# Layer 0 of a four-layer graph network: the last 20 nodes' attention weights turned by TensorE instead of by VectorE blocks and DMAs

## The chip, the cores and the metric

The kernel runs on one core of a Trainium2 chip. The metric is device time in microseconds, the median of several runs; every execution is one launch of the whole program. The engines are named as in the profile: PE is TensorE (PEld its weight loads), DVE VectorE, ACT ScalarE, POOL GpSimd, SP SyncE, which here only issues DMAs.

## The reference

A graph of 2708 nodes with 512 features each passes through four layers. Every layer is followed by a residual and a layer norm: `x = layernorm(x + layer(x, adj))`. Layer 0, the only one that the change touches, is attention with 8 heads of 64, masked by the adjacency matrix:

```python
keys    = einsum('nj,hjk->hnk', x, Wks)
queries = einsum('nj,hjk->hnk', x, Wqs)
values  = einsum('nj,hjk->hnk', x, Wvs)
atts = einsum('hqk,hmk->hqm', queries, keys) / 64**0.5
atts = softmax(atts - 1e16 * (1 - max(adj, eye)), axis=-1)
out  = einsum('hqm,hmk,hko->qo', atts, values, Wo)
```

Layers 1 to 3 are two graph convolutions and an additive graph attention. All data are float32.

## The kernel before, in words

**Tiles.** The nodes are cut into 22 chunks of 128 (`NC`), the last with 20 nodes (`LR`). Keys lie transposed in `KT`, values in `V` (128 nodes of a chunk on the partitions, 512 values in the free dimension). Layer 0 works through 85 items: for each of the first 21 chunks of queries four pairs of heads (class `Pair`), and one item (class `Last`, item 84) for the 20 queries of the last chunk with all eight heads, four groups of 32 partitions side by side. The keys of an item are taken in three batches: chunks 0 to 7, 8 to 15 and 16 to 21 (`ends`, `ND` = 16).

**The steps of an item.** `scores` (PE products into `pss`, DVE adds the mask and takes maxima into `s`), `weights` (ACT's exponential in place on `s`, with the row sums by the accumulator), and then the weights have to be turned, so that the keys lie on the partitions. For batches 0 and 1 this is done in two steps: `blocks` (two DVE transposes of 32x32 blocks from `s` into a tile `d`, L380) and `deal` (four DMAs, one for each group of 32 partitions, from `d` into a tile `e`, L390). That leaves the keys of a chunk in another order, partition 4x+i for key 32i+x, and the values of the first 16 chunks are computed in that order as well: POOL permutes x before the projection (L264). For batch 2 `turn` uses PE transposes into PSUM (`pst`, L409 to L418), copied by ACT to `pt`, `pt2` and `lastT`. `values` then multiplies with `V` (L436) into `av`, or for `Last` into four banks `avz`, and `finish` copies the result out of PSUM (L456, or L500 to `otz`) and stores it in DRAM from POOL's queue (`otd`, L457, L501).

**The order.** For PE, DVE and ACT the order is written out by hand (`manual_schedule`): in step i of the loop the newest item gets its scores, the one before (`cur`) its weights and turns, and the ones before that (`late`, `old`) their values, a batch at a time. In the step after the last item's scores, `cur` is the last item, `late` item 83 and `old` item 82. SP's and POOL's order isn't written out; a planner chooses it. Tiles `d` have two buffers, tiles `e` three; the PSUM tags `s0` and `s1` have two banks each and hold the scores' products and later `avz`.

**Behind the items.** `heads_rows` and `last_sums` turn the reciprocals of the row sums (PE `prs`, `prz`), copy them by ACT (L524, L535, one buffer `rst`) and store them from POOL (L525, L536). Then the output projection: for every chunk SP loads the stored values (`otl`, L683), x (L684) and the reciprocals (`rb`, L692), Wo having been loaded once (L113), POOL multiplies (L693), PE projects (`po`, L696), and DVE adds x (L697) and does the layer norm.

Of the kernel before, what the change touches and what calls it, by code (L numbers as in the profile page):

```python
# [8 lines left out]
F32 = mybir.dt.float32  # L9
AF = mybir.ActivationFunctionType  # L10
# [5 lines left out]
P = 128  # L16
BLK = 512
# [5 lines left out]
def kernel(  # L23
# [22 lines left out]
    nc = tc.nc  # L46
# [11 lines left out]
    def cols(b):  # L58
        return b * BLK, min(BLK, N - b * BLK)
# [11 lines left out]
    ident = const.tile([P, P], F32, tag="ident", name="ident")  # L71
# [45 lines left out]
    ends = [0, 8, 16, NC]  # L117
    ND = ends[2]
    KD4 = P // 32
# [16 lines left out]
    FILL = 32 - LR  # L136
    otd = [dram.tile([P, NP, rows(c)[1]], F32, tag=f"otd{c}", name=f"otd{c}") for c in range(NC)]
    with ExitStack() as l0:
# [12 lines left out]
        def batch(k):  # L151

            n0 = ends[k] * P
            return n0, min(ends[k + 1] * P, N) - n0
# [54 lines left out]
        with tc.tile_pool(name="kvw", bufs=1) as kvw, tc.tile_pool(name="xTb", bufs=2) as xtp, tc.tile_pool(  # L209
            name="ps_0", bufs=4, space=PSUM  # L210
# [4 lines left out]
            for b in range(NB):  # L215
                n0, w = cols(b)
# [86 lines left out]
        ps_s = l0.enter_context(tc.tile_pool(name="ps_s", bufs=2, space=PSUM, reuse_waits="tile"))  # L303
        sp = l0.enter_context(tc.tile_pool(name="sp", bufs=5, reuse_waits="tile"))
        dp = l0.enter_context(tc.tile_pool(name="dp", bufs=2, reuse_waits="tile"))
        ep = l0.enter_context(tc.tile_pool(name="ep", bufs=3, reuse_waits="tile"))
        ptp = l0.enter_context(tc.tile_pool(name="ptp", bufs=1, reuse_waits="tile"))

        class Pair:
# [58 lines left out]
            def weights(self, k):  # L368

                w = batch(k)[1]  # L370
                for j in range(2):
                    s = self.s[k][:, j, :w]
                    nc.scalar.activation(s, s, AF.Exp, bias=self.nm[j], accum_out=self.sums(j, k))  # L373

            def blocks(self, k, j):

                n = ends[k + 1] - ends[k]
                if k not in self.D:
                    self.D[k] = dp.tile([P, KD4, 2, n, 32], F32, tag="d", name=f"d{self.c}_{self.p}_{k}")
                nc.vector.transpose(  # L380
                    self.D[k][:, :, j].rearrange("p i m x -> p m i x"),
                    self.s[k][:, j, : n * P].rearrange("p (m i x) -> p m i x", i=KD4, x=32),
                )

            def deal(self, k):

                n = ends[k + 1] - ends[k]
                e = ep.tile([P, KD4, 2, n, 32], F32, tag="e", name=f"e{self.c}_{self.p}_{k}")
                for g in range(KD4):
                    nc.sync.dma_start(  # L390
                        e[:, g].rearrange("p j m x -> p (j m x)"),
                        self.D[k][32 * g : 32 * g + 32].rearrange("p i j m x -> p i (j m x)"),
                    )
                self.E[ends[k]] = e
# [30 lines left out]
            def weight(self, m, j):  # L425

                if m >= ND:
                    return self.pts[m, j]
                f = max(f for f in self.E if f <= m)
                return self.E[f][:, :, j, m - f, :]  # L430
# [28 lines left out]
        class Last(Pair):  # L459
# [19 lines left out]
            def weight(self, m, p, j):  # L479
                if m >= ND:  # L480
                    return self.pts[m, j][:, 32 * p + FILL : 32 * p + 32]
                f = max(f for f in self.E if f <= m)
                return self.E[f][:, p, j, m - f, FILL:]

            def values(self, m0, m1):
                if self.done == 0:
# [54 lines left out]
        with tc.manual_schedule(  # L541
            engines={mybir.EngineType.PE, mybir.EngineType.DVE, mybir.EngineType.Activation}
        ):
            for i in range(len(items) + 3):
# [4 lines left out]
                if i < len(items):  # L549
                    c, p = items[i]  # L550
# [559 lines left out]
    with tc.tile_pool(name="zp", bufs=2) as zp:  # L1110
# [44 lines left out]
        def banks(name):  # L1155
            return [ps_acc.tile([P, BLK], F32, tag="acc", name=f"{name}_{k}") for k in range(FC)]
# [41 lines left out]
        w = cols(TAIL)[1]  # L1198
# [22 lines left out]
        while n0 < NH * P:  # L1221
            w = min(BLK, NH * P - n0)
            n1 = NH * P + n0
            nchunks = w // P
            j = n0 // BLK
# [26 lines left out]
            m4, m7, e = banks(f"m4_{j}"), banks(f"m7_{j}"), banks(f"e0_{j}")  # L1252
# [13 lines left out]
            m3, m6, e = banks(f"m3_{j}"), banks(f"m6_{j}"), banks(f"e1_{j}")  # L1266
# [61 lines left out]
```

## Time and profile before

| | |
|---|---|
| median of 3 runs | 2588.55 us (2586.21 to 2588.58) |
| the profiled execution | 2589.45 us, its span 2587.7 us |
| PE busy | 2532.2 us, 98% of the span |
| DVE busy | 1874.8 us, 72% |
| ACT busy | 1211.7 us, 47% |
| mean granted clock of PE | 0.991 |
| layer 0's items on PE | to 1253.5 us; the output projection from 1256.6 us |

The page names engine, line, operation, output and inputs of each group; times in a timeline are from the start of the span. The square bracket at the end of a timeline's row is the idle time of the engine before it and what ended it; "issue" is waiting for nothing that the profile shows. In the windows the columns are the length of the window, then busy time and number of instructions of PE, PEld, DVE, ACT and POOL, then the granted clock, the DMA engines' mean busy share and GB/s.

### The profile page before, as it was taken

To read this page: it belongs to the slowest core of one execution; us is meant where nothing else is said; L and a number is where in the kernel's file an instruction comes from. 1 tells how busy PE (TensorE), PEld (TensorE's weight loads), DVE (VectorE), ACT (ScalarE), POOL (GpSimd) and SP (SyncE) were. 2 spreads that over 40 slices of the span, in tenths; PEclk is the share of its full clock that TensorE was granted. 3 is DMA by queue.
4 is the path that set the end of the run, shared out by engine and by line. 5 is a ranking of instruction groups with operands and counts; after the bars stand their busy time and mean duration, and the time that the engine had idled before them with its cause. 6 is when DMAs were issued, how large, how long until landed. Compare 5 with 4: busy or idle time off the path is not lost.

```text
span 2587.7 us, 42022 instructions
## 1 busy us (share of the span) xinstructions
PE 2532.2 (98%) x15263; PEld 1468.0 (57%) x15263; DVE 1874.8 (72%) x4576; ACT 1211.7 (47%) x2417; POOL 314.0 (12%) x322
## 2 busy tenths in 40 slices
PE   9999999999999999999899999899999999999997
PEld 4445676766776767676556444444444466444465
DVE  2004999999999999999484777988776874443544
ACT  2113878788787787887111001565665640000000
POOL 2110000000000000000220000343333430000000
PEclk9999999999999999999899999999999999999999
DMA  5112888888888888888763444454433213644633
GB/s 201 33 54 69 217 233 212 232 216 213 234 212 212 233 213 222 225 210 199 215 201 87 125 124 145 119 158 137 124 108 116 64 31 111 186 139 144 178 102 106
DMA packets 221499, 411.42 MB, mean 159 GB/s; under 512 B 28765, under 2 KB 48911, under 8 KB 221292
## 3 DMA queue, kind: packets, MB, share of 16 engines
q1 hardware_dynamic: 215052, 392.00, 55.5%
q0 software_dynamic: 6240, 16.73, 1.7%
q8 instruction: 121, 1.98, 0.3%
q14 instruction: 86, 0.70, 0.1%
HBM read 213.55 MB, written 16.72 MB: 89 GB/s over the span
## 4 chain that ended last, share of the span: by engine, by line
PE 79%; issue 9%; DVE 7%; DMA 2%; ACT 1%; SPq 1%; POOL 0%; POOLq 0%; DVEq 0%; ACTq 0%
PE pss L329 15%; PE av L436 15%; PE acc L750 13%; PE acc L856 7%; PE m L1160 6%; PE pf L762 3%; PE psv L269 3%; PE pst L409 3%; PE psq L230 3%; PE psk L230 2%; PE ph L842 1%; PE acc_0a L750 1%; DVE d L380 1%; DMA e<-d 1%; DVE s L351 1%
## 5 line engine op out<-in xcount | busy, mean ns | idle before, releaser
L351 DVE CUSTOM_DVE_ANT_0 s<-pss,adj 128x512 f32<-128x512 f32 (+1 forms) x1020 | 574.5, 619 | 27.3 <-PE pss L329 25.4
L373 ACT ACTIVATE s<-s,nm 128x1024 f32<-128x1024 f32 (+1 forms) x510 | 527.7, 1037 | 17.3 <-DVE nm L366 15.5
L329 PE MATMUL pss<-KT,qt 64*128 64x512 f32 (+1 forms) x2016 | 459.5, 565 | 4.0 <-DVE mx L351 3.9
L380 DVE STREAM_TRANSPOSE d<-s 128x1024 f32<-128x1024 f32 x340 | 402.4, 1222 | 9.4 <-DMA e<-d 6.5
L750 PE MATMUL acc<-pt,x 128*128 128x512 f32 (+1 forms) x880 | 336.2, 541 | 9.7 <-ACT pt L803 9.7
L436 PEld LDWEIGHTS av<-e,V 128*64 128x64 f32 x5376 | 294.6, 137 | 62.7 <-DMA e<-d 46.2
L436 PE MATMUL av<-e,V 128*64 128x128 f32 x5376 | 326.3, 274 | 0.0
L329 PEld LDWEIGHTS pss<-KT,qt 64*128 64x128 f32 x2016 | 191.1, 186 | 139.9 <-issue 67.2
L750 PEld LDWEIGHTS acc<-pt,x 128*128 128x128 f32 x880 | 159.4, 194 | 186.1 <-issue 162.8
L856 PE MATMUL acc<-at,h 128*128 128x512 f32 (+1 forms) x504 | 196.8, 543 | 0.0
L814 POOL TENSOR_TENSOR cs<-cs,pt 128x512 f32<-128x512 f32 (+2 forms) x110 | 157.6, 1433 | 202.2 <-ACT pt L803 199.8
L801 DVE TENSOR_TENSOR pt<-pt,at 128x512 f32<-128x512 f32 (+2 forms) x132 | 109.0, 833 | 76.4 <-ACT pt L800 76.2
L457 POOL DMA_DIRECT2D otd<-ot x84 | 45.3, 540 | 954.9 <-ACT ot L456 942.5
L1190 ACT ACTIVATE z<-pz,rdeg 128x512 f32<-128x512 f32 (+1 forms) x22 | 15.1, 688 | 311.5 <-PE pz L762 311.5
L93 ACT ACTIVATE ln_t<-lnve 128x1 f32<-128x1 f32 x88 | 17.7, 201 | 305.3 <-DVE lnve L107 305.2
L856 PEld LDWEIGHTS acc<-at,h 128*128 128x128 f32 x504 | 90.2, 190 | 101.4 <-issue 99.0
L410 ACT COPY pt<-pst 128x512 f32<-128x512 f32 x170 | 91.5, 589 | 120.0 <-PE pst L409 119.8
L436 PEld LDWEIGHTS av<-pt,V 128*64 128x64 f32 x1680 | 90.0, 136 | 64.6 <-ACT adj L187 46.2
L803 ACT ACTIVATE pt<-pt 128x512 f32<-128x512 f32 (+2 forms) x132 | 76.1, 579 | 102.8 <-DVE pt L802 102.6
L867 DVE SCALAR_TENSOR_TENSOR cs<-at,rdeg,cs 128x512 f32<-128x512 f32 (+2 forms) x126 | 86.2, 684 | 41.9 <-DMA at<-in_adjT_dram 40.9
L436 PE MATMUL av<-pt,V 128*64 128x128 f32 x1680 | 110.3, 278 | 1.4 <-ACT ot L456 1.4
L85 DVE COPY KT<-psk 128x512 f32<-128x512 f32 (+1 forms) x12 | 7.5, 629 | 131.6 <-PE psk L230 113.9
(299 smaller groups left out, 3563.7 us busy)
## 6 DMA issues: line engine op xcount, KB each, us to landing
e<-d SPq DMA_DIRECT2D x680, 256.0 KB
at<-in_adjT_dram SPq DMA_DIRECT2D x210, 256.0 KB
a<-in_adj_dram SPq DMA_DIRECT2D x38, 677.0 KB
adj<-in_adj_dram SPq DMA_DIRECT2D x42, 512.0 KB
at_a<-in_adjT_dram SPq DMA_DIRECT2D x40, 256.0 KB
at_c<-in_adjT_dram SPq DMA_DIRECT2D x40, 256.0 KB
at_f<-in_adjT_dram SPq DMA_DIRECT2D x40, 256.0 KB
adj<-in_adj_dram SPq DMA_DIRECT2D x21, 330.0 KB
```

The source lines that it names most:

```text
L230: nc.tensor.matmul(ps[:, :w], w_sb[:, k, p * P : (p + 1) * P], xb[:, k, :w], start=(k == 0), stop=(k == KC - 1),)
L329: nc.tensor.matmul(pss[j][:, :w], qt[h, self.p, :], KT[h, self.p, n0 : n0 + w], start=True, stop=True)
L351: nc.vector.tensor_tensor_reduce(out=s[:, j, h0 : h0 + hw], in0=pss[j][:, :hw], in1=a[:, n0 + h0 : n0 + h0 + hw], scale=1.0, scalar=LOW, o ...
L373: nc.scalar.activation(s, s, AF.Exp, bias=self.nm[j], accum_out=self.sums(j, k))
L380: nc.vector.transpose(self.D[k][:, :, j].rearrange("p i m x -> p m i x"), self.s[k][:, j, : n * P].rearrange("p (m i x) -> p m i x", i=KD4 ...
L410: nc.scalar.copy(sb, pt)
L436: nc.tensor.matmul(self.av[j * KD : (j + 1) * KD, out], V[:, m, h * KD : (h + 1) * KD], weights[j], start=(self.done == 0), stop=(self.don ...
L750: nc.tensor.matmul(acc[k][:, :w], last[0][g : g + mr, :] if m == NC - 1 else values[:mr, k * P : (k + 1) * P], moving[g : g + mr, :w], sta ...
L801: nc.vector.tensor_tensor(pt[:mr, :w], pt[:mr, :w], at[:mr, :w], ALU.subtract)
L814: nc.gpsimd.tensor_tensor(sums[:mr, :w], sums[:mr, :w], pt[:mr, :w], ALU.add)
L856: nc.tensor.matmul(acc[hc][:, :w], lastH[g : g + mr, :] if m == NC - 1 else H[m][:mr, hc * P : (hc + 1) * P], at[g : g + mr, :w], start=(m ...
L1160: nc.tensor.matmul(acc[k][:, : moving.shape[1]], combined[which, m][:, k * P : (k + 1) * P], moving, start=(m == 0), stop=(stop and m == N ...
```

## The change

Only the class `Last` changes, and in it only batches 0 and 1. `weights` lets ACT write the exponentials into a tile `d` of shape queries x 2 x chunks x 128, with key 32i+x of a chunk at place 4x+i, the order in which `V` has the values. `blocks` does nothing. `deal` issues no DMA: it transposes each 128x128 piece of `d` on PE, four to a PSUM bank (tags `s0`, `s1`), and DVE copies each bank into `e`. `weight` takes its 20 columns from the new layout. Batch 2 is as before.

```diff
                 f = max(f for f in self.E if f <= m)
-                return self.E[f][:, p, j, m - f, FILL:]
+                return self.E[f][:, j, m - f, 32 * p + FILL : 32 * p + 32]
+
+            def weights(self, k):
+
+                w = batch(k)[1]
+                n = ends[k + 1] - ends[k]
+                if ends[k] >= ND:
+                    return Pair.weights(self, k)
+                self.D[k] = dp.tile([P, 2, n, P], F32, tag="d", name=f"dz_{k}")
+                for j in range(2):
+                    nc.scalar.activation(
+                        self.D[k][:, j].rearrange("p m (x i) -> p m i x", i=KD4),
+                        self.s[k][:, j, :w].rearrange("p (m i x) -> p m i x", i=KD4, x=32),
+                        AF.Exp,
+                        bias=self.nm[j],
+                        accum_out=self.sums(j, k),
+                    )
+
+            def blocks(self, k, j):
+                pass
+
+            def deal(self, k):
+
+                n = ends[k + 1] - ends[k]
+                e = ep.tile([P, 2, n, P], F32, tag="e", name=f"ez_{k}")
+                for j in range(2):
+                    for m0 in range(0, n, 4):
+                        pt = ps_s.tile([P, BLK], F32, tag=f"s{j}", name=f"psz{k}_{j}_{m0}")
+                        for i in range(4):
+                            nc.tensor.transpose(pt[:, i * P : (i + 1) * P], self.D[k][:, j, m0 + i, :], ident)
+                        nc.vector.tensor_copy(e[:, j, m0 : m0 + 4, :], pt)
+                self.E[ends[k]] = e
```

## The prediction

> **What bounds the kernel now.** I read the page first, for the engine that carries the span.
>
> ```profile
> PE 2532.2 (98%) x15263; PEld 1468.0 (57%) x15263; DVE 1874.8 (72%) x4576; ACT 1211.7 (47%) x2417; POOL 314.0 (12%) x322
> q8 instruction: 121, 1.98, 0.3%
> ```
>
> TensorE is busy nearly everywhere, so what is gained on its path at one place stays gained. The change touches one of 85 work items, the last one of layer 0, so the question is what ends the time between 1227 and 1262 us. For that I read the chain of waits there.
>
> ```profile
> 1223.46 5.91 DMA e<-d
> 1229.50 2.38 DVE d L380 x2
> ...
> 1239.01 0.63 SPq L390
> 1239.68 2.96 SPq L113
> 1242.88 6.66 DMA otl<-otd
> 1249.62 5.57 DMA otl<-otd
> 1255.19 1.36 POOL otl L693
> 1256.59 9.10 PE po L696 x16
> ```
>
> SP's queue is full of the shuffles e<-d until 1239.64; only then does it issue Wo and the blocks for the output projection. Next, TensorE in order of time, and the granted clock microsecond by microsecond.
>
> ```profile
> 1239.74 3.71 PE L436 MATMUL avz<-e,V 128*64 128x20 f32 x121
> 1245.14 0.41 PE L436 MATMUL avz<-e,V 128*64 128x20 f32 x7 [1.69 <-issue]
> ...
> 1245.83 5.72 PE L436 MATMUL avz<-e,V 128*64 128x20 f32 x118
> 1252.65 0.83 PE L436 MATMUL avz<-e,V 128*64 128x20 f32 x10 [1.09 <-issue]
> 1256.59 19.45 PE L696 MATMUL po<-wo_sb,otl 128*128 128x512 f32 x40 [3.12 <-POOL otl L693]
> ```
>
> ```profile
> 1246.00:1247.00 1.00, 1.00 (x38) 1.00 (x38) 0.00 (x0) 0.09 (x1) 0.54 (x1) 0.95 1.01 350
> 1247.00:1248.00 1.00, 1.00 (x25) 1.00 (x22) 0.00 (x0) 0.00 (x0) 0.00 (x0) 0.50 1.17 344
> 1260.00:1261.00 1.00, 1.00 (x3) 0.53 (x2) 0.00 (x0) 0.00 (x0) 0.00 (x0) 0.72 0.00 0
> ```
>
> The last item's values stop twice for nothing a semaphore shows. The stops lie 128 matmuls apart (121 | 7 + 2 + 118 | 10), that is 256 instructions with the weight loads, and the 30526 PE instructions over the 121 packets of the q8 instruction queue (packets, MB, share) are about 252 each: these are instruction fetches, late while the DMA engines are full (share 1.0). After the first stop the clock falls to 0.50 at about 1246.9 and returns at about 1260.6. Then TensorE idles 3.12 us. POOL, in order, says why:
>
> ```profile
> 1253.94 0.52 POOL L536 DMA_DIRECT2D rz_d<-rstz  x1 [7.01 <-ACT otz L500]
> 1254.46 0.78 POOL L501 DMA_DIRECT2D otd<-otz  x1
> 1255.19 3.96 POOL L693 TENSOR_TENSOR otl<-otl,rb 128x512 f32<-128x512 f32 x3
> ```
>
> The first product for the projection stands behind two DMA issues that wait for the last item's end (ACT copies otz at 1253.56).
>
> **Removed.** Four DVE block transposes (L380, 1.22 us each; DVE has idle time there), eight DMAs of 256 KB, and SP's issues of them (1231.93 to 1239.64). So SP reaches Wo (L113) right behind item 83's shuffles, near 1229 instead of 1239.68; nothing in the trace makes Wo wait for more. Wo, three otl, three rb and three x are about 3.3 MB, issued in 13 us in the trace; they should be issued by 1242 and land by about 1245, where before they filled the engines until 1255.5.
>
> **Added, ACT.** The exponentials of batches 0 and 1 now write into the d buffers, so they wait until item 83's shuffles have read those. The trace shows when: DVE's transposes, which need the same buffers, start at 1229.50 and 1233.22 after waiting 1.84 and 1.35 us for DMA e<-d. ACT starts batch 0 at 1229.5 instead of 1227.65 and batch 1 at 1233.2 instead of 1230.07. Behind them on ACT stand the copy ot of item 82 (TensorE's av bank waits for it), the third batch and the copies pt. Four ACTIVATEs write with a step of four elements. No ACT row has that. Lower end: L373 itself, 1.14 us each with the accumulator read. Upper end: POOL's permuting copies of x (L264), 4.13 us for four with a step against 2.29 us for four straight, 1.8 times, so 2.05 us each. I take 1.14, the row of the same engine and operation; the upper end makes the item 1.9 us later (followed through the chain below). [...]
>
> **Added, PE and DVE.** 32 transposes. Row L409 has 8 in 1.02 us in the chain, so 16 per batch cost 2.05 us, all on TensorE's path. Eight DVE copies of 128x512 out of PSUM at 0.69 us (L85), 5.5 us, lie on an idle DVE beside TensorE's next work; their banks (tags s0, s1) are free after the last scores at 1227.4, and the last item's avz waits for the second batch's copies, done near 1239.0, before it starts.
>
> **TensorE step by step.** Item 82's values end at 1228.8 as now. Transposes of batch 0 from 1230.7 (first exponential) to 1232.9 (second at 1231.7, plus eight transposes). Item 83's values, 3.2 us: 1236.1 (now they start at 1230.21). Batch 1's transposes, whose exponentials are ready at 1235.5: 1238.15. Twelve pst transposes, 1.46: 1239.6. Item 83's rest, 1.75: 1241.35. The last item from pt and lastT, 2.77: 1244.1. Then 128 matmuls at 3.71/121, 3.93: 1248.05; prs and prz 0.35; 128 more, 3.93: 1252.35. Now they end at 1253.48: 1.1 us earlier, although the item's values start 4.4 us later, because the two stops and the half clock are taken out.
>
> **Behind it.** With the loads landed by 1245, POOL's first three L693 can be issued ahead of L536 and L501, as readiness orders POOL (it is not among the engines whose order is written by hand). Then the projection follows avz without the 3.12 us, and at full clock: its first 16 matmuls took 9.10 us, where 66 later ones took 28.52 us (0.432 each, 6.9 for 16), 2.2 us lost now. From there the stage is TensorE's, 176 matmuls by 0.432, so its start moves its end. Next late could be otz's copies (po1 and po2 reuse banks of avz), which only need to come within po0's 3.4 us.
>
> Sum: -1.1 - 3.1 - 2.2 = -6.4. For one late fetch in place of two I give back 0.5: -5.9. The profiled execution took 2589.45 us (span 2587.7), so it would take 2583.55; it lies 0.9 above the median of 2588.55, which goes to 2582.65, say 2582.7. A difference of 0.2%, 5.2 us, is about what a measurement of this kernel can tell from no change.
>
> [...] The trace holds no window of transposes alone: in each item 12 of them, 1.46 us, lie between other matmuls, at clock 1.00; one stop of 1.69 us among avz was enough for 0.50. In the new order TensorE idles from 1228.8 to 1230.7 and then only transposes for 2.05 us; later it transposes for 3.5 us on end. [...]
>
> **Rivals.**
> First: POOL keeps its order. L693 stays behind L501; only the 1.1 us and part of the slow start come off, and TensorE still idles about 3.2 us. For: SP and POOL are ordered by what the planner takes as ready, not by the trace. Against: the loads move about ten microseconds ahead of the two DMA issues. Time: 1 to 3 less, 2586.5.
> Second, slower: the clock falls between 1233 and 1240. At 0.50 the trace has 82 avz matmuls from 1246.95 to 1251.4, 54 ns each against 30.7; 352 of them cost 8.3 us more, and the transposes and item 83's values (5.3 us) up to 4 more if the drop comes first. avz then ends at 1260.6 to 1264, and the projection starts there cold instead of at 1256.59: 4 to 8 us slower, about 2594.5. [...]
> Third: ACT's stepped writes at 2.05 us: 1.9 us of the gain go, about 2584.5; with another step of TensorE late, less.
>
> **How the numbers follow.** Forecast case 0.48, first rival 0.24, second 0.20, third 0.08. Faster by over 0.2%: 0.85 of the forecast case (0.41), a little of the first and third (0.03): 0.44. Slower: 0.65 of the second (0.13), and 0.04 for both a late POOL and a cold clock: 0.17. The rest, 0.39, is within. Low end: the forecast with no late fetch and 3 us for later waits that an earlier start may meet better, 2579.5. High end: the second rival's nearer half, 2593. The forecast's own range is 2580 to 2585.
>
> **What would show it.** Right: SP issues Wo near 1229; avz runs without a stop at clock 1.0 and ends near 1252; L693 stands before L501 on POOL; po follows avz within 0.5 us and its first 16 matmuls take about 7 us. Wrong: PEclk 0.50 in the windows from 1233 on (second rival); L693 behind L501 with a PE gap near 3 us (first); ACTIVATEs with output d at 2 us (third). If the exponentials wait past 1233.2 because Wo's load slows item 83's shuffles, every step behind them slips by as much.

## The result and the profile after

The kernel after takes 2590.46 us (median of 22 runs, 2586.32 to 2597.29) where the kernel before, beside it, takes 2586.85 us (22 runs, 2581.12 to 2590.67). The ratio is 1.0016, 95% interval 1.001 to 1.0022: slower by 3.6 us, not faster by 5.9. (The ratio is worked out over the runs and isn't the quotient of the two medians; the same holds for the tables below.) The profiled execution of the kernel after took 2592.34 us, its span is 2590.5 us.

Two lines of the page answer to the first ones of before:

```profile
PE 2535.0 (98%) x15295; PEld 1470.1 (57%) x15295; DVE 1874.1 (72%) x4580; ACT 1214.6 (47%) x2417; POOL 313.7 (12%) x322
q8 instruction: 121, 1.98, 0.3%
```

TensorE has 32 matmuls and 32 weight loads more, the 32 turns. The instruction queue q8, which I take to bring its code, still moves 121 pieces. This will matter. In order of time, ScalarE, the queues and TensorE in the stretch that the prediction worked on (line numbers behind about 515 are 31 higher than before; this execution stands 1.95 us behind that of before already at 1221, where the two programs are still the same, so 1.95 is to be taken off each start):

```profile
1231.55 2.09 ACT L493 ACTIVATE dz<-s,nm 128x1024 f32<-128x1024 f32 x1 [1.86 <-DMA e<-d]
1235.90 2.19 ACT L493 ACTIVATE dz<-s,nm 128x1024 f32<-128x1024 f32 x1
```

```profile
1233.70 3.65 PE L512 MATMUL psz<-ident,dz 128*128 128x128 f32 x16 [2.91 <-ACT dz L493]
1237.28 1.31 PE L436 MATMUL av<-pt,V 128*64 128x128 f32 x20
...
1240.48 1.97 PE L512 MATMUL psz<-ident,dz 128*128 128x128 f32 x16
...
1248.26 3.89 PE L436 MATMUL avz<-ez,V 128*64 128x20 f32 x128
...
1252.43 3.92 PE L436 MATMUL avz<-ez,V 128*64 128x20 f32 x128
1256.66 5.82 PE L727 MATMUL po<-wo_sb,otl 128*128 128x512 f32 x13 [0.32 <-issue]
```

Batch 0's exponentials start when item 83's shuffles give the d buffers back, as foreseen; the row of batch 1's shows no such wait, ScalarE only comes to it then. Each takes 2.1 us and not 1.14. TensorE stands still for 2.91 us ahead of the first turned batch, and turns it in 3.65 us where the second takes 1.97. The windows say why (us, busy times and counts by engine, then the granted clock, the DMA share and GB/s):

```profile
1229.00:1233.00 4.00, 1.78 (x32) 1.54 (x30) 0.61 (x4) 2.14 (x4) 0.00 (x0) 1.00 0.86 239
1233.60:1236.80 3.20, 3.07 (x13) 2.67 (x14) 1.38 (x2) 3.06 (x6) 0.54 (x1) 0.50 0.88 246
1237.00:1256.00 19.00, 19.00 (x468) 18.17 (x467) 4.77 (x10) 7.36 (x18) 2.91 (x4) 1.00 0.55 156
```

After the stop the clock is at 0.50 for 3.41 us, from 1233.46 to 1236.87, then at 1.00 through avz. In the clock records of this profile and of that of before every fall that ends within the span lasts 3.41, 6.83 or 13.65 us, and the starts of the falls of one record lie whole multiples of 3.413 us apart; such a stretch of 3.41 us is called a window of the clock below. SP's issue of Wo and, of POOL, the last item's issues beside the products for the projection:

```profile
1231.47 0.61 SPq L113 DMA_DIRECT2D wo_sb<-in_wo_dram  x1
1253.54 1.28 POOL L724 TENSOR_TENSOR otl<-otl,rb 128x512 f32<-128x512 f32 x1
1255.41 0.55 POOL L567 DMA_DIRECT2D rz_d<-rstz  x1 [0.59 <-ACT otz L531]
1256.87 0.74 POOL L532 DMA_DIRECT2D otd<-otz  x1 [0.91 <-ACT otz L531]
```

So most of what was foreseen came: Wo issued early, avz without a stop, the projection 0.32 us behind it and at full clock. From 1221 to the start of layer 1 (1367) this execution gains 4.2 us on that of before. By 2383, in layer 3, it is only 0.3 us ahead, with falls of the clock in layers 1 and 2 at other places than before (1666.9, 1728.4, 1824.0 and 2100.4 us; there 1653.1, 1670.2, 1731.6, 2008.1 and 2100.2), and there it loses 2.8 us at one spot, where the order of the instructions is the same. TensorE there, in the kernel before and in the kernel after:

```profile
2393.00 1.99 PE L1160 MATMUL m<-jb,x 128*128 128x512 f32 x4 [1.64 <-DVE jb L1152]
```

```profile
2393.82 3.65 PE L1191 MATMUL m<-jb,x 128*128 128x512 f32 x4 [2.79 <-DVE jb L1183]
```

The stop is 1.15 us longer and the four matmuls behind it run at half clock. VectorE's wait for the block at_c is behind it, before and after:

```profile
2392.05 0.29 DVE L1147 TENSOR_TENSOR at_c<-at_c,ident 128x128 f32<-128x128 f32 x1 [1.97 <-DMA at_c<-in_adjT_dram]
```

```profile
2392.87 0.29 DVE L1178 TENSOR_TENSOR at_c<-at_c,ident 128x128 f32<-128x128 f32 x1 [3.11 <-DMA at_c<-in_adjT_dram]
```

And the DMA queues between 2388 and 2393 (packets, MB, share of 16 engines), before and after:

```profile
q1 hardware_dynamic: 660, 1.20, 77.4%
q0 software_dynamic: 80, 0.26, 13.1%
```

```profile
q1 hardware_dynamic: 611, 1.10, 72.7%
q0 software_dynamic: 80, 0.26, 13.4%
q8 instruction: 1, 0.02, 1.8%
```

One piece of q8 travels beside at_c in the kernel after (from 2389.4 on, for 1.45 us), and none in the kernel before. That became the theory, called C in the texts below; A and B are told in the first of them.

To compare executions, the tables below give two differences to the first profile of the kernel before, each between the starts of the same VectorE instruction. The stretch goes from item 83's last score blocks (1221.0 there) to layer 1's first h (1367.2). The spot goes from a sum y of layer 3 (2382.9) to the product jc (2405.4). Less than zero is a gain. A further profile of the kernel before gives -2.0 and -0.4, so 2 us in the stretch between two single profiles are no finding.

### The profile page after: what moved, and what is told of

It is laid out like the page before. It is cut to its first block, busy times and chain, and to the rows that moved or that the text cites. A ratio compares the mean times of both kernels' runs of the same rounds, so it can differ in the third digit from the quotient of the medians.

```text
span 2590.5 us, 42086 instructions
## 1 busy us (share of the span) xinstructions
PE 2535.0 (98%) x15295; PEld 1470.1 (57%) x15295; DVE 1874.1 (72%) x4580; ACT 1214.6 (47%) x2417; POOL 313.7 (12%) x322
## 3 DMA queue, kind: packets, MB, share of 16 engines
q8 instruction: 121, 1.98, 0.3%
## 4 chain that ended last, share of the span: by engine, by line
PE 80%; issue 9%; DVE 6%; DMA 2%; ACT 1%; SPq 1%; POOL 0%; POOLq 0%; DVEq 0%; ACTq 0%
PE pss L329 15%; PE av L436 15%; PE acc L781 13%; PE acc L887 7%; PE m L1191 6%; PE pf L793 3%; PE psv L269 3%; PE pst L409 3%; PE psq L230 3%; PE po L727 3%; PE psk L230 2%; PE ph L873 2%; DVE s L351 1%; DVE d L380 1%; DMA e<-d 1%
## 5 line engine op out<-in xcount | busy, mean ns | idle before, releaser
L380 DVE STREAM_TRANSPOSE d<-s 128x1024 f32<-128x1024 f32 x336 | 397.6, 1221 | 8.0 <-DMA e<-d 3.0
```

The lines of the kernel that those rows point to most:

```text
L380: nc.vector.transpose(self.D[k][:, :, j].rearrange("p i m x -> p m i x"), self.s[k][:, j, : n * P].rearrange("p (m i x) -> p m i x", i=KD4 ...
```

## The experiments

All kernels of a batch ran on one chip together with the kernel before.

### The two kernels again, and the two halves of the wait

The kernel before again and the kernel after again; the exponentials in the score buffers, so that they don't wait for item 83's shuffles; and the exponentials written straight, without the values' order, so that the last 20 nodes' weights meet the wrong values:

```
-self.D[k] = dp.tile([P, 2, n, P], F32, tag="d", name=f"dz_{k}")
+self.D[k] = sp.tile([P, 2, n, P], F32, tag="s", name=f"dz_{k}")      # third run

-self.D[k][:, j].rearrange("p m (x i) -> p m i x", i=KD4),
-self.s[k][:, j, :w].rearrange("p (m i x) -> p m i x", i=KD4, x=32),
+self.D[k][:, j].rearrange("p m x -> p (m x)"),                      # fourth run
+self.s[k][:, j, :w],
```

> The kernel before once more, for its spread and for a second profile of it. Theory A (the clock's windows): the stretch of the last item is faster by 4 to 5 us in the changed kernel, but what follows then lies otherwise against fixed windows of 3.41 us, and more of the 2-us stops of layers 1 to 3 end in half clock. If the windows are fixed to the start of the execution, this profile shows the half clock at the same places as the first one (1247, 1653, 1670, 1731, 2008, 2100 us, give or take 1); if they run free, at others. Theory B (the stretch itself): the stretch of the last item is slower in most executions than in the one profiled, and the rest does not matter. Both: ratio 1.000, within 0.001.

> The changed kernel once more. Both: 1.001 to 1.002 of before. A: from item 83's values to the first layer norm of layer 1 it gains 4 to 5 us on the kernel before again, and it has lost 4 us or more against that by the end, at places where the granted clock is 0.50 in this kernel and 1.00 in the kernel before. B: the stretch gains less than 1 us or loses, and from there to the end the two kernels run alike within 1 us.

> The exponentials go into tiles of the tag s, which are free by then, and not into the d buffers, which item 83's shuffles still read. ACT starts batch 0 behind the copies of item 83 (1.9 us earlier), TensorE's stop before the first transposes falls from 2.9 to about 1 us and its clock stays at 1.00 there; the stretch ends 2 to 3 us earlier than in the changed kernel. B: the total falls by the same 2 to 3 us, to 1.0004. A: the total changes by that and by what the windows then do, anything from -6 to +3 us against the changed kernel.

> The exponentials are written in the order in which they are read; the 20 last nodes' weights then meet the wrong values, so this one's output is not the reference's. It takes the step of four elements away. ACT's four ACTIVATEs take 1.14 us instead of 2.1; batch 0's second one ends 1 us earlier, and the stretch ends 1 to 2 us earlier than in the changed kernel. B: the total falls by 1 to 2 us. A: by that and by what the windows do, -5 to +4 us.

| kernel | median us (runs) | ratio, interval | stretch | spot |
|---|---|---|---|---|
| before again | 2586.11 (11) | 0.9993, 0.9985 to 1.0002 | -2.0 | -0.4 |
| after again | 2589.59 (11) | 1.0009, 1.0 to 1.0018 | +0.3 | +3.2 |
| score buffers | 2590.80 (12) | 1.0004, 0.9992 to 1.0016 | -5.8 | +2.6 |
| straight | 2587.31 (11) | 0.9997, 0.9988 to 1.0006 | -5.2 | +2.8 |

The kernel before had a median of 2587.42 beside them. Its second profile has half clock from 1243.6, 1666.9 and 1728.3 on and none at 1653, 2008 or 2100, where the first has it: the falls differ between executions of one kernel. The second profile of the kernel after gains nothing in the stretch: half clock lies there at 1233.9 for two windows, at 1257.8 and at 1339.7. Written straight, the exponentials take 1.15 us, so the step makes the 2.1. With either half of the wait gone the stretch gains what was foreseen, 5 to 6 us, in the profile. Yet the medians don't show it, and the profiles of the kernel after and of both versions lose 2.6 to 3.2 us at the same spot of layer 3. The twelve times with the score buffers fall into two groups, five of 2582.7 to 2586.6, the profiled one among them, and seven of 2589.8 to 2595.4. Every execution has its mean granted clock on record, also without a profile: 0.994 to 0.995 in the five, 0.989 to 0.993 in the seven.

### Is the spot a matter of code? Idle instructions

The 30,590 matmuls and weight loads of TensorE over the 121 pieces of row q8 (1.98 MB, each recorded with 16,384 bytes) make 253 for a piece; with the 468 records of TensorE that wait or drain, 256 stand between one piece and the next on the mean. That the pieces are TensorE's is read from this count; a second instruction queue (q14, 0.70 MB in 86 pieces) moved nothing from 15 us ahead of the spot to its end in the first profiles of the two kernels. If that reading is right, an added instruction moves every later fetch. Idle matmuls (their results are overwritten) change that count; in this kernel one such float32 matmul of the program is two matmuls and two weight loads in the profile, four instructions (48 of them are the x96 below), and a turn is one of each (the change's 32 are the 32 and 32 above):

```
 # ahead of the first turned batch; with 24 ahead of each half in the score buffers, or 8
+nc.tensor.matmul(pt[:, :20], ident, ident[:, :20], start=True, stop=True)   # x48
 # kernel before, ahead of the first projection matmul
+nc.tensor.matmul(po[:, :20], ident, ident[:, :20], start=True, stop=True)   # x16
```

> The kernel after, with 48 idle fp32 matmuls of 20 columns (192 TensorE instructions, results overwritten) in front of the first turned batch, where TensorE stands still for 2.5 to 2.9 us. Together with the 64 instructions that the change itself adds this makes 256, and the profile's instruction queue brings TensorE's code in pieces of 16,384 bytes, one for every 256 TensorE instructions. Theory C (the change moves the places where code is fetched: one piece lands at 2389.3 in the kernel after, inside the transfer of at_c that layer 3 waits for, and at 2353 and 2401 in the kernel before): the fetches of layers 1 to 3 go back to where they were in the kernel before, the stop ahead of jb at about 2392 is 1.3 to 1.7 us and not 2.8 to 3.1, no half clock at 2394, and 2.4 to 2.9 us of the later loss are gone; with TensorE kept busy up to the turned batch the half clock at 1233 goes too, so about 2585 us. Theory A (the later losses come only from when layer 3 arrives against the clock's grid of 3.41 us): the stop ahead of jb stays at 2.8 us, and the total moves only by what the stretch gains (2587 to 2588). Theory B (the cost is in the stretch 1221 to 1262 alone): it gains 2 us at 1262, nothing at 2394.

> The kernel before, with 16 idle fp32 matmuls of 20 columns (64 TensorE instructions) in front of the first projection matmul, where TensorE stands still for 3.1 us anyway: as many instructions as the change adds, and nothing else of the change. Theory C: a code fetch at about 2388 to 2390, the stop ahead of jb 2.5 to 3.1 us, half clock behind it, so 2.4 to 2.9 us lost between 2383 and 2405 as in the kernel after; median about 2589.5. Theories A and B: nothing of that; the stop stays at 1.3 to 1.7 us, median 2587 (within 1 us of the kernel before).

> The kernel after with the exponentials in the score buffers (as in the third run) and with 2 x 24 idle fp32 matmuls of 20 columns (192 TensorE instructions) ahead of the two halves of the first turned batch, whose stops are 1.0 and 0.9 us: some 1 us longer there. Theory C: no long stop ahead of jb (1.3 to 1.7 us), so the stretch's gain of about 5.5 us stays: median 2582 to 2584, faster than both kernels. Theory A: stop of 2.8 us ahead of jb, 2585 to 2588. Theory B: as the third run, 2588 to 2591.

> The same with 2 x 8 idle matmuls (64 TensorE instructions, 128 with the change's own): the code fetch that fell into the transfer of at_c should come some 12 us earlier than in the kernel after. Theory C: the fetch at about 2370 (in this kernel's earlier time), ahead of the transfer, stop ahead of jb 1.3 to 1.7 us, median 2581 to 2584, unless the moved fetches meet another transfer that is waited for. Theories A and B: as for the run with 192.

| kernel | instructions beside before | median us | ratio, interval | stretch | spot |
|---|---|---|---|---|---|
| after, 192 idle | 259 | 2597.68 | 1.0056, 1.0042 to 1.007 | +8.4 | -0.2 |
| before, 64 idle | 64 | 2588.87 | 1.0016, 1.0007 to 1.0025 | +3.1 | -0.4 |
| score buffers, 192 idle | 259 | 2600.76 | 1.006, 1.0048 to 1.0073 | +10.0 | -0.1 |
| score buffers, 64 idle | 131 | 2588.60 | 1.0014, 1.0004 to 1.0024 | -4.2 | -0.5 |

The kernel before had 2585.12 beside them. (5 runs each with 192 idle, 11 each with 64. The kernel after itself has 67 more: 64 for the turns and 3 that wait.) The loss at the spot is gone wherever the count is another. But the medians fail, in the first three because I mis-sized the fill; TensorE in the first of them:

```profile
1227.51 15.86 PE L513 MATMUL psz<-ident 128*128 128x20 f32 x96
```

An idle matmul with a fresh 128x128 weight took 0.11 us at full clock and 0.21 at half clock, not the 0.03 of avz, so the fill overran the stop by 13 us. The clock was at 0.50 for four windows from 1232.8 on in spite of it, 5.3 us after the fill began (0.67 on the mean of 1227.5 to 1243.2). In the fourth the stretch still gains 4.2 us; its profile is of an execution of 2585.09, and the four of its eleven up to 2585.11 have a clock of 0.994 to 0.996, the others 0.990 to 0.994.

The kernel before with 64 was a miss: I expected the loss there, and its stop ahead of jb was 1.14 us. Its fetch came at 2395.9, just behind that wait, which ended at 2394.63. The kernel after has three instructions more, the waiting ones. That gave the sharpest test: one idle matmul more, 68 instructions instead of 64.

### 68 instead of 64, and turns in place of matmuls

The kernel before with 17 idle matmuls for 16; and, in the stop, idle turns of the 128x128 identity: 40 in the kernel after, 2 x 15 with the score buffers, 2 x 12 with the score buffers and the step on the side that ScalarE reads:

```
+nc.tensor.transpose(pt[:, :P], ident, ident)     # x40; x15 and x15; x12 and x12
-self.D[k][:, j].rearrange("p m (x i) -> p m i x", i=KD4),
-self.s[k][:, j, :w].rearrange("p (m i x) -> p m i x", i=KD4, x=32),
+self.D[k][:, j],                                 # fourth run
+self.s[k][:, j, :w].rearrange("p (m i x) -> p m x i", i=KD4, x=32),
```

> [...] Two things are tried at once and can be read apart in the trace. Clock: the fill of 192 instructions with 20 columns was followed by four windows at half clock from 1232.8; theory G (the gate takes matmuls of 20 columns for idleness, those of 128 columns for work): no half clock between 1231 and 1262, so 2 to 3.5 us less at 1262 than in the kernel after. Rival: the stop's fill does not matter, half clock at about 1233 as in the kernel after. Code: 144 instructions more than the kernel before; theory C: the fetch that fell at 2389 comes 15 us earlier, the stop ahead of jb is 1.0 to 1.6 us, no half clock at 2394, 2.5 to 2.9 us less between 2383 and 2405. Both: median 2584 to 2586; neither: 2590.

> [...] Theory G: no half clock from 1228 to 1262 in any but few runs, the second group of times (2590 to 2595 of the third run) goes; with theory C the loss at 2394 goes too: median 2580 to 2583, faster than both kernels by 0.15 to 0.3%. If 20-column matmuls of the values themselves (avz, 7.8 us) still bring the clock down in some runs, the two groups stay, each 2.5 us lower: median about 2586.

> The run of the kernel before with 64 idle instructions, with one matmul more (68 instructions): the kernel after has the 64 instructions of its turns and 3 waiting instructions more, so its pieces of code end 67 instructions earlier than those of the kernel before; with 64 the fetch came just behind the wait for jb (at 2395.9). Theory C: with 68 it comes ahead of that wait, at 2390 to 2392, the stop ahead of jb is 2.5 to 3.1 us (1.14 with 64), and 2 to 2.9 us are lost between 2383 and 2405. Rival (the stop depends on the change itself, or on when layer 3 arrives): 1.1 to 1.6 us, nothing lost there.

> As the second of these, with the order of the values made on the side that the ScalarE instruction reads (every 32nd score, 128 bytes apart) and the exponentials written straight, and with 2 x 12 idle turns. If it is the stepped write alone that makes 2.1 us of 1.14, the four exponentials take 1.14 to 1.3 us, there is no stop ahead of the turned batches, and the median is 1 to 2 us below the second's (2579 to 2582). If any stepped side costs that, 2.1 us and the second's time.

| kernel | instructions beside before | median us | ratio, interval | stretch | spot |
|---|---|---|---|---|---|
| after, 40 turns | 147 | 2588.00 | 1.0008, 0.9997 to 1.0018 | -1.8 | -0.4 |
| score buffers, 30 turns | 127 | 2585.82 | 1.0001, 0.9992 to 1.001 | -5.3 | -0.4 |
| before, 68 idle | 68 | 2594.33 | 1.0022, 1.0011 to 1.0033 | +2.7 | +2.9 |
| score buffers, step read, 24 turns | 115 | 2584.97 | 1.0, 0.9986 to 1.0014 | -6.1 | -0.3 |

The kernel before had 2586.34. The stop ahead of jb in the kernel before, with 64 idle instructions and then with 68:

```profile
2394.63 1.55 PE L1163 MATMUL m<-jb,x 128*128 128x512 f32 x3 [1.14 <-DVE jb L1155]
```

```profile
2400.09 3.63 PE L1163 MATMUL m<-jb,x 128*128 128x512 f32 x4 [2.70 <-DVE jb L1155]
```

With 68 the fetch came at 2396.2, ahead of the wait's end at 2400.09. Four instructions in layer 0 make 1.56 us of stop and half clock in layer 3, in a kernel without the change. Of the 19 profiles, the five that have 67 or 68 more instructions lose 2.6 to 3.2 us at the spot, with stops of 2.51 to 3.12 us ahead of jb; all others lose nothing, with stops of 1.05 to 1.64. That settles what decides the spot. How a piece of 16,384 bytes holds up at_c, whose wait was 1.14 us longer, isn't shown.

The step on the reading side costs the same:

```profile
1229.73 2.12 ACT L493 ACTIVATE dz<-s,nm 128x1024 f32<-128x1024 f32 x1
```

Turns took 0.11 us each (40 in 4.58 us), so 40 overran the stop too, but the clock stayed at 1.00 from 1230 to 1242.

### Where the rest goes

Without the loss at the spot the versions still came out beside the kernel before and not below it. Three runs fill the stops at the starts of layer 2's blocks, where the clock had fallen in 12 of the 14 profiles until then, with the same turns, in the kernel before, with the score buffers (and 2 x 12 turns), and in the kernel after:

```
 pt = softmax2(b, m)
+if b > 0 and m == m0:
+    turns(acc[0], 18 if b < NB - 1 else 8)       # so many idle turns of ident
```

> The kernel before, with 80 idle turns of the identity (160 TensorE instructions of 0.11 us) in the five stops of TensorE at the starts of layer 2's blocks (18 ahead of the blocks 1 to 4, whose stops are 2.1 to 2.4 us, and 8 ahead of the last, 1.05 us). The granted clock falls in some of these stops in every profile (1731, 2008 and 2100 in the first profile of the kernel before), at 1.4 to 3 us each. Expected of both theories: none or nearly none of these falls, 2 to 4 us less than the kernel before: 2582 to 2585, the lowest to the highest time closer together than 10 us; if the fill changes nothing, 2586.

> The version with the exponentials in the score buffers and 2 x 12 idle turns ahead of the halves of the first turned batch, with the same fills of layer 2. Theory A: as much below the filled kernel before as the stretch gains, 3 to 5 us: 2578 to 2582. Theory B: within 1 us of the filled kernel before, as the version without the fills was of the kernel before (2585 against 2586.3).

> The kernel after with the same fills of layer 2 and nothing else: the 160 instructions also move the code fetch away from the place at 2389, so 2.8 us of loss go with them. Theory A: 5 to 7 us below the kernel after (2583 to 2585) and within 1 us of the filled kernel before or below it. Theory B: the distance to the filled kernel before is the kernel after's (3.6 us) less 2.8, so 1 us above it, and the spread stays.

| kernel | median us | ratio, interval | stretch | spot |
|---|---|---|---|---|
| before, layer 2 filled | 2586.38 | 0.9995, 0.9987 to 1.0004 | -2.5 | -0.5 |
| score buffers, 24 turns, layer 2 filled | 2588.80 | 1.0006, 0.9994 to 1.0017 | +1.9 | -0.4 |
| after, layer 2 filled | 2584.96 | 0.9991, 0.9982 to 1.0 | -2.8 | -0.1 |

The kernel before had 2586.91. Filling layer 2 gave it only 0.5 us, not 2 to 4: its profile gains 3.1 us on the first one of the kernel before within layer 2's blocks and then loses 2.6 at the start of layer 3, where the clock falls at 2165.7, at a stop of 1.79 us, and in none of the other profiles. The kernel after came out 1.4 us below the filled kernel before, on theory A's side, but the two intervals overlap, so this doesn't decide between A and B; the 160 turn instructions took the spot's loss away too. The score buffers came out above, as neither theory has it. Their profile shows a case that I had not counted, TensorE within avz:

```profile
1244.10 2.03 PE L436 MATMUL avz<-ez,V 128*64 128x20 f32 x64
1247.43 2.98 PE L436 MATMUL avz<-ez,V 128*64 128x20 f32 x64 [1.30 <-issue]
1250.92 7.02 PE L436 MATMUL avz<-ez,V 128*64 128x20 f32 x128
```

```profile
1248.30:1261.80 13.50, 13.18 (x176) 10.57 (x173) 0.07 (x3) 1.11 (x6) 5.62 (x6) 0.50 0.05 9
```

TensorE stops for 1.30 us among the last item's values, for code as I read it (a piece of q8 travels from 1244.8 to 1246.2, and the stop begins at 1246.1), and the clock is at 0.50 for the next four windows, as for three to five in every profile of the kernel before (13.65 us in the first). The 128 matmuls behind it take 7.02 us and not 3.9. Its stretch ends at +1.9 where executions with nearly the same layer 0 (30 turns; step read, 24 turns) reach -5 to -6. The twelve times of this version fall into two groups, 2578.2 and 2579.2, and 2586.6 to 2592.8, which fits one event of some 8 us; that all of the slower ones had this one wasn't seen, for only one was profiled. Their clocks part in the same way: 0.996 in the two, 0.991 to 0.993 in the ten. From the score buffers on, every profile of a changed layer 0 is of an execution at or below its version's median, by up to 5.9 us. So the stretches of -4 to -7 show better than the median execution, and that is why the medians don't follow them.

The last two runs are the kernel after with as many turns as fit into the stop (24), and the score buffers without turns in layer 0, with layer 2 filled:

> The kernel after with 24 idle turns (48 TensorE instructions, 24 x 0.11 = 2.7 us) in the stop of 2.5 to 2.9 us ahead of the first turned batch; 40 turns took 4.6 us and overran it by 1 to 2 us, and the median was 2588.0 at 2586.3 of the kernel before. If the cost in layer 0 is the half clock behind the stop: no half clock at 1231 to 1240, no loss at 2394, 1262 reached 4 us earlier against 1221 than in the kernel before, median 1 to 2 us below the run with 40 (2586 to 2587 beside 2586.5 of the kernel before). If it is the wait itself, which stays: as the run with 40, 2588.

> The version with the exponentials in the score buffers and the fills of layer 2, without idle turns in layer 0: as the kernel after with the fills of layer 2 (2585.0, 2 us below the kernel before), less the stop of 2.8 us ahead of the first turned batch, which becomes 1.0 and 0.9 us. If nothing else decides: 2582 to 2583.5, a ratio of 0.998 to 0.999, faster than both kernels. If code comes late to avz in most executions (as with the 24 turns, where 10 of 12 times lay at 2586.6 to 2592.8): two groups, 2579 to 2581 and 2586 to 2592, and a median of 2585 to 2588.

| kernel | median us | ratio, interval | stretch | spot |
|---|---|---|---|---|
| after, 24 turns | 2585.01 | 0.9993, 0.9982 to 1.0004 | -4.2 | -0.4 |
| score buffers, layer 2 filled | 2584.02 | 0.9996, 0.9982 to 1.0009 | -6.9 | -0.5 |

TensorE and the windows in the first:

```profile
1230.35 2.84 PE L513 MATMUL psz<-ident 128*128 128x128 f32 x24
1233.39 1.09 PE L515 MATMUL psz<-ident,dz 128*128 128x128 f32 x8 [0.20 <-ACT dz L493]
1235.38 1.09 PE L515 MATMUL psz<-ident,dz 128*128 128x128 f32 x8 [0.90 <-ACT dz L493]
```

```profile
1229.00:1233.00 4.00, 4.00 (x50) 3.78 (x46) 0.24 (x4) 2.17 (x3) 0.00 (x0) 1.00 0.95 218
1233.60:1236.80 3.20, 2.30 (x24) 1.89 (x24) 2.01 (x4) 3.20 (x4) 0.54 (x1) 1.00 0.92 296
```

24 idle turns, which compute nothing, make the kernel after, 3.6 us slower than the kernel before, into one that can't be told from it (1.1 us below its 2586.16). They leave the wait for the d buffers and the 2.1-us exponentials where they were, so the loss doesn't come from the wait itself. They take away both the half clock behind the stop and the fetch at the spot, which cost 2.8 and 3.2 us in the two profiles of the kernel after; the shares of the two in the median aren't parted by this run. The lowest median is that of the second, 2584.02, between the two cases expected; the interval of its ratio holds 1, so no version is shown to beat the kernel before. Five are below the kernel after's 2590.46 by over 4 us, though on other chips.

## Why the prediction was wrong, by its steps

- **The removed DMAs** held. SP issues Wo at 1231.47, which is 1229.5 on the clock of before, where 1229 was said, and avz runs without a stop in this profile. (The lines of before have the stops 127 matmuls apart, 7 + 2 + 118, and not 128; with the weight loads that is 254 instructions, and a piece of q8 travels from 1242.9 and one from 1250.1 on, ahead of the stops at 1243.4 and 1251.6, so the reading as fetches stands.)
- **The exponentials' starts** held in the main: 1231.55 and 1235.90, less 1.95, are 1229.6 and 1233.95, for 1229.5 and 1233.2; the second is late because the first pair took longer.
- **The exponentials' length** was the first mis-sized term: 2.1 us for 1.14. The upper bound from POOL's stepped copies, 2.05, was right and I took the lower one. The runs give 0.95 us an instruction (2.09 for 1.14), and the same for a step on the reading side (2.12).
- **TensorE step by step** therefore slipped. The first turned batch starts at 1231.75 (less 1.95) for 1230.7, and its stop, 2.91 us, brought the half clock that I had put into the second rival, with a loss of 1.7 us on the turns (3.65 for 1.97) and not of 4 to 8. The clock was back at 1236.9, before item 83's values began (1237.28), so not through them. avz ends at 1254.4 for 1252.35, 0.9 us later than before and not 1.1 earlier. The projection starts 1.9 us earlier than before, and with its full clock that makes the 4.2 us of this profile.
- **Turns alone** did not bring the clock down here. In the run with 40 turns, these and the 16 of the first batch fill 6.3 us from 1230.14 on without another matmul, and the clock stays at 1.00 from 1230 to 1242. In the kernel after the clock fell at 1233.5, within the stop and ahead of the first turn at 1233.70, and one window later, in which only turns had run, it was back; in two further profiles with this layer 0 it took two windows, the second with item 83's values in it.
- **The projection** held: the first of POOL's three products (now L724) goes ahead of the last item's two DMA issues, and po follows 0.32 us behind avz at full clock.
- **The two stops taken off** were sized from one execution. 1.69 and 1.09 us there; in the second profile of the kernel before 0.31 and 0.35; in the three further runs that have its layer 0 up to there (64 and 68 idle instructions, layer 2 filled) one of 2.41, 2.57 and 2.04. Half clock followed in all five. The stretch of the second profile is 2.0 us shorter and that with layer 2 filled 2.5, so part of the forecast gain was a difference between executions. Nor are such stops gone for good with the change, as the one of 1.30 us shows.
- **What failed above all** is the sentence that what is gained on TensorE's path at one place stays gained. The change added 67 instructions to TensorE, and I counted their time and not their place in the program. They moved a code fetch of layer 3 into a transfer that TensorE waits for there: 2.8 to 3.2 us. The stretch gained less than that: its mean is -1.5 in the three profiles with the layer 0 of before (0, -2.0, -2.5) and -2.2 in the three with that of the kernel after (-4.2, +0.3, -2.8), so 0.7 us where 5.9 were forecast. Together that makes 2.1 to 2.5 us of the 3.6; where the other 1.1 to 1.5 lie isn't known.

What stays open is where the clock falls in executions without a profile; only its mean is known there. In the profiles layer 2's fills took the falls at its blocks away, but in the kernel before most of the gain was lost again in layer 3.

## What to carry to other kernels

Count the instructions that an edit adds to an engine, not only their time: 67 more here moved the fetches of TensorE's code behind them, and the one that fell into a transfer that is waited for went with a loss of 2.6 to 3.2 us, as much as a small edit gains. Where such an edit moves the time against its sign, change the count alone (four idle instructions were enough here), and compare the traces far behind the edit before explaining it from the edit. A stop of 2.5 to 3 us that can't be removed can be filled with idle turns of full width, no longer than the stop (24 took 2.84 us here, and the clock stayed at 1.00). Where executions of one kernel spread by some 10 us, compare a profile's own time and mean clock with the median before a gain is read from it.

## What was not expected of the hardware

- Row q8 moved 121 pieces of 16,384 bytes, one for about 253 matmuls and weight loads of TensorE; I read them as its code. With 68 idle instructions in place of 64 one of them came ahead of the end of a wait and not behind it, and 2.9 us were lost at that place.
- In the clock records of the first profiles of the two kernels the 14 falls that end within the span last 3.41 us (ten), 6.83 (three) or 13.65 (one). Half clock followed stops of 2.51 to 3.12 us in all eight cases ahead of jb and of the first turned batch; after stops of 1.05 to 1.64 us ahead of jb it never did.
- A ScalarE exponential of 128x1024 takes 2.1 us with a step of 16 bytes on its output or of 128 bytes on its input, and 1.14 to 1.15 straight.
- Idle matmuls of 20 columns with a fresh 128x128 weight took 0.11 us each at full clock, as long as turns of 128 columns. During 96 of the first the clock fell, though TensorE was busy throughout; 40 of the second held it at 1.00.
